# Linear attention's reciprocals: spread over the heads' rows by a matmul, or loaded with repeats

## The chip, the cores and the metric

The kernel runs on one core of one Trainium2 chip. The metric is the device time of one execution in microseconds (us), the median of several runs. The engines of the core are named as in the profile: PE (TensorE, matmul), PEld (its weight loads), DVE (VectorE), ACT (ScalarE), POOL (GpSimd), SP (SyncE, which here only issues DMAs).

## What is computed

A decoder layer on x of 2 x 2048 rows by 512: linear attention, cross attention to 154 context rows, and a mixture of 8 experts of which 6 are used, plus a shared one. Each part is normalised ahead and added to x. The change touches the end of the first part:

```python
q_proj = _elu1(jnp.einsum('bhnd,hdf->bhnf', q, proj_matrix))
k_proj = _elu1(jnp.einsum('bhnd,hdf->bhnf', k, proj_matrix))
kv = jnp.einsum('bhnf,bhnd->bhfd', k_proj, v)
attn = jnp.einsum('bhnf,bhfd->bhnd', q_proj, kv)
k_sum = k_proj.sum(axis=2)
z = 1.0 / (jnp.einsum('bhnf,bhf->bhn', q_proj, k_sum) + 1e-08)
attn = attn * z[..., None]
out = attn.transpose(0, 2, 1, 3).reshape(b, n, d)
return out @ w_out + b_out
```

There are 16 heads of 32 columns. For each head and token there is one denominator, and its reciprocal z multiplies that head's 32 numerators.

## The kernel before

The 4096 rows are cut into 8 blocks of 512 tokens (`TB`); blocks 0 to 3 are the first batch (`bpb` is 4), 4 to 7 the second. A tensor of a block is held transposed, as 4 chunks of 128 columns (4 heads of 32) by 512 tokens. Large products are made of pairs, a high part that the matmul takes exactly and a low rest, as three matmuls (`product`, L144). `low` (L116) makes the rest by a subtraction.

SBUF is handed out by pools. `big` has 17 buffers of 8 KB per partition (`eight`), which hold weights, loaded queries (`qst`), numerators (`num`), the attended pairs (`at`), and so on; `work` has among others 4 buffers `hl` for pairs (`pair_of`). PSUM has 8 banks: 4 in pool `ps` (`bank`), for products of all kinds, and 4 in pool `sc`, for features and scores. A scheduler of the tile framework puts the instructions of each engine in an order when the kernel is built; engines and DMA queues then work in that order, and a tile that takes over a buffer waits for the last reader of the one before. Nearly all DMAs are issued by SP; the numerators and the cross attention's keys by POOL.

The stages that matter here:

- The loop at L1306 makes the key features of all blocks, and, two steps behind, the query features, numerators and denominators of blocks 0 to 3. `numerators` (L485) stores those of blocks 0 to 3 to DRAM (`numd`), while those of blocks 4 to 7 stay in SBUF. In block 7 of this loop the cross attention's weights, w_out, the first numerators and the first reciprocals are loaded.
- The loop at L1346 goes over the 16 chunks of blocks 4 to 7 (`steps`): it loads queries (`load_queries`), makes their features (matmul `pqp`, then Relu and Exp on ACT and a sum on DVE: `features`, L361), numerators (`pn`) and denominators (`pd`). Between them it deals out the finishing of blocks 0 to 6: `ahead` gives each step a block and a pair of chunks, for which `attended` is called, two calls a step. After a block's last chunk its `attention_out` (L567) is added to the fill work: four times 12 matmuls `po_a`, an addition of x's rows (`xr_a`) and a store to x1.
- The loop at L1390 is the cross attention of all blocks (scores `psc`, Exp on ACT). In its first block, block 7 of the linear attention is finished in the same way.
- The experts follow, from about 1075 us to the end.

The way of a denominator: `denominators` (L507) sums into one bank `pd` per block; `reciprocals` (L522) adds 1e-8 on DVE (`den`), stores it to DRAM (`dd`, four DMAs), loads it back over 128 partitions (`z`, `turned`), takes the reciprocal there and stores it to DRAM again (`zd`, `stored`). `load_reciprocals` (L548) then loads for two chunks, by four DMAs, each head's row 32 times into the 32 partitions of that head (`zr`, in an `hl` buffer). `attended` (L558) multiplies the numerators by it on POOL, in place (the trace names that operation num<-num,zr), copies the result to the high part on ACT, and makes the low part on DVE.

Of the kernel before, what the change touches and what calls it, by code (L numbers as in the profile page):

```python
# [17 lines left out]
P = 128  # L18
# [12 lines left out]
Z_EPS = 1e-8  # L31
LAG = 3
SC = 4
GROUP = 2


@with_exitstack
def decoder_layer(
# [59 lines left out]
    def eight(shape, dtype, name):  # L98
        return big.tile(shape, dtype, tag="b8", name=name)
# [4 lines left out]
    def pair_of(name, n=TB):  # L104
        return work.tile([P, 2, n], FR, tag="hl", name=name, bufs=4)
# [361 lines left out]
        dense.add(*tr[:1], query_chunk(b, 0), *ln[3:], *tr[1:2], key_chunk(b, 3))  # L467
        dense.add(*tr[2:3], query_chunk(b, 1), *tr[3:], query_chunk(b, 2), query_chunk(b, 3))

    qsts, qps, pds, nums, numd, zrs, zds, ats = {}, {}, {}, {}, {}, {}, {}, {}  # L470

    def load_queries(b, c):
        qsts[b, c] = eight([3 * HD, 4, TB], FR, f"qst{b}_{c}")
# [48 lines left out]
    def reciprocals(b, pd):  # L522

        den = half(f"den{b}")
        nc.vector.tensor_scalar(den, pd, Z_EPS, None, ALU.add)
        dd = dram.tile([4, NC, TB], F32, name=f"dd{b}")
        for h in range(4):
            nc.sync.dma_start(out=dd[h], in_=den[h * HD : h * HD + NC, :])
        z = small.tile([P, H * TB // P], F32, tag="z", name=f"z{b}", bufs=1)
        flat = "h c n -> (h c n)"  # L530
        zd = dram.tile([4, NC, TB], F32, name=f"zd{b}")

        def turned():
            nc.sync.dma_start(out=z, in_=dd.rearrange(flat).rearrange("(p n) -> p n", p=P))

        def stored():
            tc.keep_in_program_order(nc.vector.reciprocal(z, z))
            nc.sync.dma_start(out=zd.rearrange(flat).rearrange("(p n) -> p n", p=P), in_=z)

        dense.after(10, turned)  # L540
        dense.after(26 if b < nblk - 1 else 24, stored)
        zds[b] = zd
# [2 lines left out]
        nums[b] = eight([P, NC, TB], F32, f"num{b}")  # L545
        nc.gpsimd.dma_start(out=nums[b], in_=numd[b])

    def load_reciprocals(b, c):  # L548
        two = pair_of(f"zr{b}_{c}").bitcast(F32)
        for h in range(4):  # L550
            nc.sync.dma_start(
                out=two[h * HD : (h + 1) * HD],
                in_=zds[b][h : h + 1, c : c + 2].to_broadcast([HD, 2, TB]),
            )
        for i in range(2):
            zrs[b, c + i] = two[:, i]

    def attended(b, c):  # L558

        if c == 0:  # L560
            ats[b] = [eight([P, NC, TB], FR, f"at{b}_{i}") for i in range(2)]
        at = nums[b][:, c]
        nc.gpsimd.tensor_tensor(at, at, zrs.pop((b, c)), ALU.mult)
        nc.scalar.copy(ats[b][0][:, c], at)
        low(ats[b][1][:, c], at, ats[b][0][:, c])

    def attention_out(b, t):  # L567
        if not 0 <= b < nblk:
# [737 lines left out]
    for n in range(nblk * per):  # L1306
        b, c, t = n // per, n // NT % NC, n % NT
        dense.fill(58 if n == 0 else fl(n, 9.25) if n < 32 else fl(n, 9.5))
        if (b, c, t) == (nblk - 1, 0, 0):
            context_load()  # L1310
        if (b, c, t) == (nblk - 1, 1, 0):
            xwk = split_weight(wk_t, "xwk")
            dense.add(*(context_key(i, xwk) for i in range(NC)))
        if (b, c, t) == (nblk - 1, 2, 0):
            xwv = split_weight(wv_t, "xwv")
            bvr = half("bvr")
            nc.sync.dma_start(out=bvr, in_=bv.to_broadcast([P, D]))
            for bt in range(batches):
                dense.add(*(context_value(bt, at, xwv, bvr) for at in range(0, keys, P)))
        if (b, c, t) == (nblk - 1, 3, 0):  # L1320
            load_numerators(0)
            load_reciprocals(0, 0)
            bout = load_row(b_out, "bout")
        dense.until(stks, (b, c))
        key_features(b, c, t)
        todo.append((b, c, t))
        m = n - bpb * per - shift
        if m == -4:
            load_queries(0, 0)
        if m >= 0:  # L1330
            query_step(m)
        if n % 2 and len(todo) > LAG:
            sums_step(m)
# [12 lines left out]
    for n in range(len(steps) + 1):  # L1346
        if n < len(steps):
            b, c = steps[n]
            if n + 1 < len(steps):
                load_queries(*steps[n + 1])  # L1350
        if n + 1 in ahead:
            load_reciprocals(*ahead[n + 1])
        if n == 7:
            ln, tr = layernorm(x1[0], 0, 0, qts, "x")
            dense.add(*ln[:3])
            ln = ln[3:]
        if n == 8:
            dense.add(*tr[:1], *ln, *tr[1:])
        if n == 11:
            dense.add(*(cross_query(0, i) for i in range(NC)))  # L1360
        for i in range(2):
            if n < len(steps):
                query_features(b, c, 2 * i)
                query_features(b, c, 2 * i + 1)
            dense.fill(fl(2 * n + i, 13 if n < 12 else 14))
            if n in ahead:
                attended(ahead[n][0], ahead[n][1] + i)
                if ahead[n][1] and i:
                    whole = ahead[n][0]
                    if whole < nblk - 2:  # L1370
                        dense.add(*attention_outs(whole))
                    if whole + 1 < bpb:
                        load_numerators(whole + 1)
            if n and i:
                columns.batch()
                numerators(*steps[n - 1])
                denominators(*steps[n - 1])
        if n == 10:
            xwq = split_weight(wq_t, "xwq")
        if n == 11:  # L1380
            open_early.clear()
            attending.close()
            res = attending.enter_context(tc.tile_pool(name="res", bufs=1))
            for i in range(NC):
                load_keys(0, i)
# [4 lines left out]
    for n in range(len(steps) + LAG + 1):  # L1390
        if n < len(steps):
            b, c, t = steps[n]
            k = NT * c + t
            dense.until(xsts, (b, c))
            scores(b, c, t)
            if b == 0:
                if k == 0:
                    load_values(0)
                if k in (NC - 1 + 0, NC + 1 + 0):
                    load_reciprocals(nblk - 1, k - 0 - NC + 1)  # L1400
                if NC + 0 <= k < 2 * NC + 0:
                    attended(nblk - 1, k - NC - 0)
                if k == 8:
                    bor = load_row(bo, "bor")
                    xwo = split_weight(wo_t, "xwo")
            if b == 0 and k == 0:
                ln, tr = layernorm(x1[1], 1, 0, qts, "x")
                outs = [[attention_out(nblk - i, t) for t in range(NT)] for i in (2, 1)]
                new = [cross_query(1, i) for i in range(NC)]
                kinds = {"L": ln, "a": outs[0], "T": tr, "b": outs[1], "q": new}  # L1410
                dense.add(*(kinds[x].pop(0) for x in "LLLaTLTaTTaaqbqbqbqb"))
            if k == LAG + 0 and b:
                outs = [cross_out(b - 1, i) for i in range(NT)]
                new = [cross_query(b + 1, i) for i in range(NC)]
                if b + 1 < nblk:
                    ln, tr = layernorm(x1[b + 1], b + 1, 0, qts, "x")
                    kinds = {"L": ln, "o": outs, "T": tr, "q": new}
                    dense.add(*(kinds[x].pop(0) for x in "LLLoTLTTToqoqoqq"))
                else:
                    dense.add(outs[0], tr[0], ln[3], outs[1], *tr[1:])  # L1420
            if b == nblk - 1 and k == 1:
                ln, tr = expert_ahead(0)
                dense.add(*ln[:3])
                load_unit(0)
            if b == nblk - 1 and k == 9:
                ln, tr = expert_ahead(1)
                ready = products(0)
                dense.add(prepare(0, 0), *ln[:3], tokens_part(0, 0), tokens_part(0, 1))
                dense.add(tr[0], ready[0], ln[3], *tr[1:], ready[1], *outs[2:])
            dense.fill(fl(k, 9.5 if b == 0 else 7.75 if b < nblk - 1 else 5.5))  # L1430
            if b % bpb == bpb - 1 and b + 1 < nblk and c > 0 and t == 1:
                load_keys(b // bpb + 1, c - 1)
            if b % bpb == 0 and b and k == 0:
                load_keys(b // bpb, NC - 1)
        if LAG <= n < len(steps) + LAG:
            turn(*steps[n - LAG])
        if n > LAG:
            b, c, t = steps[n - LAG - 1]
            if t == NT - 1:
                values(b, c)  # L1440
                if c == NC - 1 and (b + 1) % bpb == 0 and b + 1 < nblk:
                    load_values((b + 1) // bpb)
# [180 lines left out]
```

## Time and profile before

| what | value |
|---|---|
| median of 3 runs | 2324.54 us (2317.61 to 2330.41) |
| the profiled execution | 2323.77 us, its span 2321.7 us |
| busy, share of the span | PE 2234.2 us (96%), DVE 72%, POOL 53%, ACT 47% |
| bytes moved | 498.23 MB, 215 GB/s over the span |
| stretch 430 to 480 us | PE busy 41.8 of 50 us, granted clock 0.90, DMA engines 94% busy |
| stretch 480 to 660 us | PE busy 159.7 of 180 us, granted clock 0.96, DMA engines 89% busy |
| stretch 660 to 720 us | PE busy 58.4 of 60 us, granted clock 0.99, DMA engines 74% busy |
| stretch 720 to 1075 us | PE busy 336.3 of 355 us, DMA engines 58% busy |
| stretch 1075 to 2322 us | PE busy 1227.4 of 1247 us, DMA engines 62% busy |

The loop over the 16 chunks (L1346) runs from about 495 to 645 us, with its loads beginning at about 445 us; the experts are over half of the span. A row of the profile that names a group of instructions gives its line, engine, operation, and the tiles written and read (out<-in); a helper's line, such as L118 for `low`, stands for all its callers, so tile names tell them apart. An arrow in a table of waits points at what ended the wait.

### The profile page before, as it was taken

How to read it: one execution, taken by the hardware profiler on the slowest of the kernel's cores; microseconds unless marked ns; L12 is line 12 of the kernel's file. 1: busy time of each engine (PE TensorE's matmuls, PEld its weight loads, DVE VectorE, ACT ScalarE, POOL GpSimd, SP SyncE). 2: the span in 40 equal slices, each digit the busy share in tenths (PEclk: the TensorE clock that was granted, in tenths of full speed). 3: DMA queues.
4: the chain of work that ended last, by engine and by line, in shares of the span. 5: the costliest groups of instructions: out<-in, count | busy, mean ns of one | idle time of the engine just before them, and what ended most of it. 6: DMA issues, size and time to landing. Idle time of an engine off the chain costs nothing.

```text
span 2321.7 us, 35182 instructions
## 1 busy us (share of the span) xinstructions
PE 2234.2 (96%) x11978; PEld 1733.5 (75%) x11978; DVE 1675.2 (72%) x2733; ACT 1101.6 (47%) x2598; POOL 1225.3 (53%) x1078
## 2 busy tenths in 40 slices
PE   7999999898989999999999999999999999999999
PEld 5888777645667777766787877888878888788887
DVE  6554555568587777878877776788787887877777
ACT  4555677656466676765343343222433223432221
POOL 5555333446475565554766454555474554755443
PEclk9999999989999999999999999999999999999999
DMA  7656777889975665666867557665547666575553
GB/s 213 182 169 176 201 219 215 248 235 278 249 216 153 171 183 170 183 183 223 287 237 260 216 185 292 226 232 226 195 168 281 231 231 235 196 281 204 209 190 132
DMA packets 201809, 498.23 MB, mean 215 GB/s; under 512 B 27738, under 2 KB 47578, under 8 KB 181694
## 3 DMA queue, kind: packets, MB, share of 16 engines
q1 hardware_dynamic: 199902, 489.89, 64.2%
q0 software_dynamic: 1728, 6.09, 0.9%
q8 instruction: 96, 1.57, 0.3%
q14 instruction: 83, 0.68, 0.1%
HBM read 351.30 MB, written 144.60 MB: 214 GB/s over the span
## 4 chain that ended last, share of the span: by engine, by line
PE 73%; DMA 12%; DVE 6%; issue 3%; ACT 2%; POOL 2%; SPq 1%; DVEq 0%; ACTq 0%; POOLq 0%
PE pg L1082 30%; PE pf L1195 11%; PE pf L148 4%; PE pk L148 3%; PE pv L148 3%; PE pq L148 3%; PE po_x L148 3%; PE xpq L148 2%; PE pp L402 2%; PE pc L745 1%; PE pkv L230 1%; PE psc L693 1%; DMA qst<-qd 1%; PE xpt L725 1%; ACT xe L703 1%
## 5 line engine op out<-in xcount | busy, mean ns | idle before, releaser
L1082 PE MATMUL pg<-xo,wq 128*128 128x512 f32 x3360 | 823.2, 393 | 3.4 <-DVE xo L118 1.4
L1082 PEld LDWEIGHTS pg<-xo,wq 128*128 128x128 f32 x3360 | 630.4, 188 | 143.0 <-DVE xo L118 3.4
L407 POOL TENSOR_TENSOR kacc<-kacc,e_k 128x512 f32<-128x512 f32 x128 | 166.0, 1297 | 225.4 <-DVE e_k L366 206.3
L1216 DVE TENSOR_TENSOR sum<-sum,pf 128x512 f32<-128x512 f32 x376 | 251.2, 683 | 45.9 <-PE pf L1195 41.3
L703 ACT ACTIVATE xe<-psc,nb 128x154 f32<-128x154 f32 x512 | 195.2, 417 | 87.5 <-DVE nb L700 81.7
L708 POOL TENSOR_TENSOR xe<-xe,sm 128x616 f32<-128x616 f32 x128 | 157.7, 1237 | 93.6 <-DVE sm L707 61.3
L1195 PE MATMUL pf<-ht,wdo 128*128 128x512 f32 x696 | 185.5, 393 | 4.9 <-DVE sum L1216 3.2
L1145 POOL TENSOR_TENSOR u<-u,gr 128x512 f32<-128x512 f32 x48 | 65.1, 1356 | 227.3 <-DVE u L1114 226.6
L366 DVE SCALAR_TENSOR_TENSOR e_k<-pp,e_k 128x512 f32<-128x512 f32 x128 | 87.4, 684 | 108.5 <-ACT e_k L365 102.4
L1113 ACT ACTIVATE u<-u 128x512 f32<-128x512 f32 x80 | 50.6, 633 | 231.6 <-DVE u L1102 231.5
L1195 PEld LDWEIGHTS pf<-ht,wdo 128*128 128x128 f32 x696 | 130.8, 188 | 35.7 <-issue 3.3
L1195 PE MATMUL pf<-hb,wdo 128*128 128x512 f32 x522 | 146.8, 398 | 1.0 <-DVE sum L1216 0.9
L148 PE MATMUL pf<-wd,hp 128*128 128x512 f32 x528 | 135.1, 403 | 5.4 <-DVE mv_n L248 3.4
L148 PEld LDWEIGHTS pf<-wd,hp 128*128 128x128 f32 x528 | 100.2, 192 | 34.6 <-issue 6.5
L700 DVE TENSOR_REDUCE nb<-psc 128x2 f32<-128x308 f32 x256 | 111.3, 464 | 12.0 <-PE psc L693 11.8
L703 ACT ACTIVATION_READ_ACCUMULATOR xe<-psc,nb 128x1 f32 x512 | 118.3, 231 | 0.0
L1102 DVE TENSOR_TENSOR u<-u,pg 128x512 f32<-128x512 f32 x160 | 107.9, 680 | 13.5 <-PE pg L1082 12.5
L1195 PEld LDWEIGHTS pf<-hb,wdo 128*128 128x128 f32 x522 | 97.2, 188 | 24.8 <-DVE sum L1216 3.6
L364 ACT ACTIVATE e_k<-pp 128x512 f32<-128x512 f32 x128 | 76.8, 601 | 69.5 <-PE pp L402 62.5
L693 PE MATMUL psc<-xkst,xst 96*128 96x154 f32 x512 | 91.8, 286 | 11.7 <-ACT xe L703 10.8
L693 PEld LDWEIGHTS psc<-xkst,xst 96*128 96x128 f32 x512 | 77.7, 193 | 27.1 <-ACT xe L703 18.0
L402 PEld LDWEIGHTS pp<-pst,kst 96*128 96x128 f32 x512 | 76.1, 192 | 27.8 <-issue 5.8
(285 smaller groups left out, 5118.7 us busy)
## 6 DMA issues: line engine op xcount, KB each, us to landing
wq<-wqs SPq DMA_DIRECT2D x90, 1024.0 KB
wqs<-wq SPq DMA_DIRECT2D x30, 1024.0 KB
wdo<-wds SPq DMA_DIRECT2D x29, 1024.0 KB
kst<-kd SPq DMA_DIRECT2D x96, 256.0 KB
qst<-qd SPq DMA_DIRECT2D x96, 256.0 KB
xst<-xqd SPq DMA_DIRECT2D x96, 256.0 KB
wdo<-wds SPq DMA_DIRECT2D x29, 768.0 KB
kd<-khl SPq DMA_DIRECT2D x32, 512.0 KB
```

The source lines that it names most:

```text
L148: nc.tensor.matmul(dst, lhsT=a, rhs=b, start=n == 0, stop=n == len(todo) - 1)
L366: nc.vector.scalar_tensor_tensor(e, src, 0.0, e, ALU.max, ALU.add)
L402: nc.tensor.matmul(pp[:, h], lhsT=stks[b, c][:, h, rows], rhs=pst[:, head], start=True, stop=True)
L407: nc.gpsimd.tensor_tensor(acc, acc, kp, ALU.add)
L693: nc.tensor.matmul(psc[:, i], lhsT=xsts[b, c][:, h, t * P : (t + 1) * P], rhs=ksts[bt, c][:, h, :], start=True, stop=True,)
L700: nc.vector.tensor_reduce(nb[:, two], psc, AX.X, ALU.max, negate=True)
L703: nc.scalar.activation(e[:, h, :], psc[:, i], AF.Exp, bias=nb[:, h : h + 1], accum_out=sm[:, h : h + 1],)
L708: nc.gpsimd.tensor_tensor(e, e, sm.unsqueeze(2).to_broadcast([P, 4, keys]), ALU.mult)
L1082: nc.tensor.matmul(pb, lhsT=w[:, p, i, k, :], rhs=xop[:, q, k, :], start=first and m == 0, stop=m == len(todo) - 1, skip_group_check=True,)
L1102: nc.vector.tensor_tensor(dst, dst, pb, ALU.add)
L1195: nc.tensor.matmul(banks[i], lhsT=w[:, p, i * P : (i + 1) * P], rhs=t[q], start=new and m == 0, stop=m == len(TERMS) - 1, skip_group_check ...
L1216: nc.vector.tensor_tensor(dst, dst, banks[i], ALU.add)
```

## The change

The reciprocals are no longer loaded with repeats. `stored` makes a pair of them, high and low part, and stores both (`zd` is twice as large). One DMA per block (`load_reciprocals`) brings the block's 2 x 16 rows of 512 tokens to 32 partitions of a new buffer `spread`, in one of 3 places that take turns. `spread` also holds, written once by `spread_setup`, a matrix of zeros and ones that says which rows belong to which of the 128 columns of a chunk. `attended` begins with one matmul by it, which puts each head's reciprocal (high plus low part) on its 32 rows of a bank `pz` of pool `ps`; DVE multiplies the numerators by that bank, ACT copies the high part as before, and POOL makes the low part. The numerators of a first-batch block are loaded two blocks ahead (block 1's together with block 0's), where it was one.

```diff
-        z = small.tile([P, H * TB // P], F32, tag="z", name=f"z{b}", bufs=1)
+        zhl = small.tile([P, 2, H * TB // P], FR, tag="z", name=f"z{b}", bufs=1)
+        z = zhl[:, 1].bitcast(F32)
...
-        zd = dram.tile([4, NC, TB], F32, name=f"zd{b}")
+        zd = dram.tile([2, 4, NC, TB], F32, name=f"zd{b}")
...
             tc.keep_in_program_order(nc.vector.reciprocal(z, z))
-            nc.sync.dma_start(out=zd.rearrange(flat).rearrange("(p n) -> p n", p=P), in_=z)
+            nc.scalar.copy(zhl[:, 0], z)
+            low(zhl[:, 1], z, zhl[:, 0])
+            nc.sync.dma_start(
+                out=zd.rearrange("r h c n -> r (h c n)").rearrange("r (p n) -> p r n", p=P),
+                in_=zhl.bitcast(F32),
+            )
...
-    def load_reciprocals(b, c):
-        two = pair_of(f"zr{b}_{c}").bitcast(F32)
-        for h in range(4):
-            nc.sync.dma_start(
-                out=two[h * HD : (h + 1) * HD],
-                in_=zds[b][h : h + 1, c : c + 2].to_broadcast([HD, 2, TB]),
-            )
-        for i in range(2):
-            zrs[b, c + i] = two[:, i]
+    spread = []
+
+    def spread_setup():
+        both = eight([P, 1 + SPREAD, TB], FR, "spread")
+        nc.gpsimd.memset(both.bitcast(F32), 0.0)
+        rows = [
+            ident[: 2 * H, r * H : (r + 1) * H]
+            .rearrange("p (h c) -> p c h", h=4)
+            .unsqueeze(3)
+            .to_broadcast([2 * H, NC, 4, HD])
+            for r in range(2)
+        ]
+        to = both[: 2 * H, 0].rearrange("p (c h d) -> p c h d", c=NC, h=4)
+        nc.vector.tensor_tensor(to, *rows, ALU.add)
+        spread.append(both)
+
+    def load_reciprocals(b):
+        nc.sync.dma_start(
+            out=spread[0][: 2 * H, 1 + b % SPREAD].bitcast(F32),
+            in_=zds[b].rearrange("r h c n -> (r h c) n"),
+        )
...
+        pz = bank(f"pz{b}_{c}")
+        nc.tensor.matmul(
+            pz,
+            lhsT=spread[0][:, 0, c * P : (c + 1) * P],
+            rhs=spread[0][:, 1 + b % SPREAD],
+            start=True,
+            stop=True,
+        )
         at = nums[b][:, c]
-        nc.gpsimd.tensor_tensor(at, at, zrs.pop((b, c)), ALU.mult)
+        nc.vector.tensor_tensor(at, at, pz, ALU.mult)
         nc.scalar.copy(ats[b][0][:, c], at)
-        low(ats[b][1][:, c], at, ats[b][0][:, c])
+        low(ats[b][1][:, c], at, ats[b][0][:, c], nc.gpsimd)
...
             load_numerators(0)
-            load_reciprocals(0, 0)
+            load_numerators(1)
+            spread_setup()
+            load_reciprocals(0)
+            load_reciprocals(1)
...
-        if n + 1 in ahead:
-            load_reciprocals(*ahead[n + 1])
+        if n + 1 in ahead and not ahead[n + 1][1] and ahead[n + 1][0] > 1:
+            load_reciprocals(ahead[n + 1][0])
...
-                    if whole + 1 < bpb:
-                        load_numerators(whole + 1)
+                    if whole + 2 < bpb:
+                        load_numerators(whole + 2)
...
-                if k in (NC - 1 + 0, NC + 1 + 0):
-                    load_reciprocals(nblk - 1, k - 0 - NC + 1)
+                if k == NC - 1:
+                    load_reciprocals(nblk - 1)
```

More of the change, by code (lines that the diff above doesn't have):

```diff
@@ L33 @@
 SC = 4
+SPREAD = 3
 GROUP = 2
@@ L468, in decoder_layer @@
         dense.add(*tr[2:3], query_chunk(b, 1), *tr[3:], query_chunk(b, 2), query_chunk(b, 3))
-    qsts, qps, pds, nums, numd, zrs, zds, ats = {}, {}, {}, {}, {}, {}, {}, {}
+    qsts, qps, pds, nums, numd, zds, ats = {}, {}, {}, {}, {}, {}, {}
     def load_queries(b, c):
```

## The prediction

> **What bounds the kernel now.** I read the page first, then a table of stretches, then the chain of waits and the waits themselves in the stretch that the change touches. The page says that TensorE (PE) is busy for 96% of the span, so a change can only gain where PE is not. The table of 20 us stretches finds that place. Its columns are the stretch, its length, the busy us (and instructions) of PE, PEld, DVE, ACT and POOL, the granted PE clock, the busy share of the DMA engines, and GB/s.
>
> ```profile
> 460.00:480.00 20.00, 16.62 (x133) 10.63 (x132) 13.60 (x22) 14.89 (x30) 7.36 (x7) 0.83 0.99 282
> 480.00:500.00 20.00, 17.99 (x89) 7.54 (x88) 12.37 (x22) 7.63 (x15) 10.08 (x9) 0.91 0.76 220
> 520.00:540.00 20.00, 17.00 (x85) 10.12 (x83) 14.70 (x22) 11.47 (x21) 10.31 (x8) 0.97 0.95 278
> 620.00:640.00 20.00, 18.07 (x93) 12.48 (x93) 9.18 (x15) 9.02 (x17) 2.53 (x2) 1.00 1.04 283
> 640.00:660.00 20.00, 12.98 (x76) 8.86 (x69) 16.13 (x36) 10.93 (x46) 10.51 (x13) 0.87 0.68 176
> 660.00:680.00 20.00, 20.00 (x120) 16.73 (x122) 16.14 (x33) 12.52 (x52) 17.47 (x14) 0.96 0.72 213
> 460.00:660.00 200.00, 176.36 (x932) 107.50 (x931) 141.42 (x227) 116.46 (x241) 104.90 (x98) 0.94 0.90 249
> ```
>
> Between 460 and 660 us PE is idle for 200 - 176.4 = 23.6 us while the DMA engines are 90% busy and no other compute engine is above 71%. The clock loses more: one minus the granted clock, times PE's busy time, summed over the ten stretches, is 9.3 us (2.8 of it in the first). From 660 us on PE is full again. So some 33 us are open here, and DMA is the suspect. The chain of waits over these 200 us (whose line the view cuts off) agrees, and the waits name what is late (us in total, times, longest):
>
> ```profile
> by line: issue 13.4%; DMA qst<-qd 9.0%; DMA zr<-zd 8.3%; DMA xr_a<-in_x 6.8%; DMA xst<-xqd 6.6%; DMA x<-xr_a 6.3%; DMA num<-numd 4.7%; DVE at L118 4.3%; PE xpq L148 4.2%; POOL num L563 3.6%; DMA zd<-z 2.5%; DVE xr_a L315 2.5%; DMA dd<-den 2
> ACT at L564 <- POOL num L563: 33.2, 15, 6.7
> POOL num L563 <- DMA zr<-zd: 27.7, 4, 17.0
> DVE at L118 <- ACT at L564: 22.9, 6, 7.7
> POOL num L563 <- DMA num<-numd: 17.6, 3, 8.8
> PE pqp L479 <- DVE e_q L366: 8.1, 6, 2.8
> zr<-zd SPq DMA_DIRECT2D x60, 128.0 KB
> ```
>
> The reader is to see a relay: POOL's multiplication waits for the reciprocals (zr) or the numerators (num), ACT's copy waits for POOL, and behind ACT's copy in its queue stand the Exp and Relu of the features (e_q), whose banks PE waits for. The last line, from the DMA issues between 430 and 660 us, counts 60 loads of zr: 7.9 MB of the 57.9 MB moved there.
>
> **The change part by part.** All sums are against the profiled execution, span 2321.7 us, 2323.8 with what lies around it; the median of the runs, 2324.5, is 0.7 above that. I add the differences to the median.
>
> *Added on PE.* 32 matmuls pz (8 blocks of 4), 128x512 like those of po_a. A dozen of these takes 2.80 us:
>
> ```profile
> 664.66 2.80 PE po_a L148 x12
> ```
>
> That is 0.233 us each from start to start, so 32 x 0.233 = 7.5 us, on PE's path since nothing else runs there meanwhile. Each pz also takes one of the four banks of `ps`. The nearest row is pn, which shares them: its weight loads waited 2.1 us in 4 cases for the bank of an out (DVE xr_a), for 16 pn. For 32 pz that is 4.2 us at most; PE itself was idle for 0.5 us of it, so 1.0. I take 1.0, ends 0 and 4.2.
>
> *Swapped.* Per chunk POOL's multiplication (mean 1422 ns there) and DVE's subtraction (mean 1134 ns) become DVE's multiplication out of a bank (DVE xr_a L315, also out of a bank: 674 ns) and POOL's subtraction (POOL's wout_lo, the same operation: 1293 ns). DVE is relieved by 32 x 0.46 = 14.7 us, POOL by 4. The relay itself is 1.42 + 0.62 + 1.13 = 3.2 us before and 0.23 + 0.67 + 0.62 + 1.29 = 2.8 after: no gain taken on the path. POOL's subtraction stands in a queue with the additions xr_a, which waited 24.1 us for their loads; a late one now holds back the low half, and po_a after it.
>
> *Setup.* One memset of 128x2048 on POOL (kacc's: 1890 ns) and one DVE operation on 32 rows (under 0.68 us), near 445 us. POOL is idle for 4.3 us there before its next kacc: cost nothing; without that cover 1.9 us. Per block there is one ACT copy and one DVE subtraction of 128x64 more (the reciprocal of that shape takes 548 ns): 8 x about 1.1 us, not on PE's path but in the chain from den to pz, which is costed under the rivals.
>
> *Removed.* 64 loads of zr, 8 of 64 KB come instead. Of the 57.9 MB, 7.9 - 0.3 (spread) - 0.2 (zd doubled) = 7.4 MB or 12.7% go away. The gain has three parts, each with both ends. First, zr's own share of the chain, 8.3% of 200 = 16.6 us, at three places (462, 588 and 636 us). A small load stands there instead: xkst, 77 KB, lands in 3.4 us, so 3 x 3.4 = 10.2 and the gain is 6.4 (0 to 16.6). Second, the numerators two blocks ahead: 4.7% of 200 = 9.4; their megabyte has to move all the same, num1's now at 445 us beside w_out's loads where the DMA share is 0.97, so I take half, 4.7 (0 to 9.4). Third, the other transfers of the chain (qst, xr_a, xst, x, zd: 31.2% or 62.4 us) go through a queue that carries 12.7% less: 7.9 us if its rate alone sets them, and half, 4.0, as many are set by the order of SP's queue (0 to 7.9). Together 15.1 of the 23.6 us of idle time. What is late next are the features' banks (8.1 us of waits for e_q) and xr_a.
>
> *Clock.* After idle spells the granted clock falls: in 475 to 479 us PE was busy 3.0 of 4 us, with one gap of 1.2 us, and the next 4 us got 0.71. So idle time given back gives back clock: 9.3 x 15.1 / 23.6 = 6.0 us (0 to 9.3).
>
> The Trainium skill speaks against this term: its page "TensorE: Matmul & The Clock Gate" (Part 1, the HAM clock gate) says that the clock is halved only after an idle window of about 3.4 us. No gap of PE between 460 and 660 us is that long (the longest has 3.1 us), so by the rule the term would be nothing and the time some 2318. The row above shows losses after shorter gaps, and I go by the row.
>
> *Buffers.* `spread` and the second numerator hold 2 of the 17 slots of `big`. In the changed order of instructions each qst's slot comes free 21 to 43 us of PE work ahead of its use, before 26 to 54; its load takes some 6 us. Nothing taken.
>
> Sum: +7.5 + 1.0 - 15.1 - 6.0 = -12.6 us: 2324.5 - 12.6 = 2312. Best end: all of PE's idle time and clock, 32.9, less 7.5: 2299.
>
> **The rivals.**
> *No change to speak of.* The idle time stays and moves to other releasers: the page shows DVE and ACT in the same relay, and SP's queue hands out loads in order, whoever is fast. For it: PE's own idle time is written mostly to e_q, not to zr. Against it: these e_q are late behind ACT's copy, which waits for POOL and so for zr. With the three gains at a third (5.0, clock 2.0): 2324.5 + 8.5 - 7.0 = 2326; its range is 2313 to 2336.
>
> *Slower: PE stops at pz.* Before, a late reciprocal stopped POOL, and PE met it only at po_a. Now pz stands in PE's own queue, and everything behind it waits: the next features, scores and outs. Block 5's den was made at 574.2 us and POOL began on its reciprocals at 593.8: 19.6 us. In the changed order PE's work between the last pd and the first pz, at the row's prices, is 50, 40, 23.3, 22.2 and 15.4 us for blocks 3 to 7. If the chain grows by 5 us (zd<-z is 5.0 us of it, at 582 us in the chain of waits, and becomes twice as large), it is 24.6, and PE waits 1.3 + 2.4 + 9.2 = 12.9 us, and some 3.5 more by the clock (three times 4 us at 0.71). With no relief of the queue this gives 2324.5 + 8.5 + 16.4 = 2349, with half of it 2339. It decides from a chain above about 23 us. Against it: zd's store shares the queue that is relieved, and block 7 has scores on ACT in its stretch (four Exp per tile, each 0.42 us and 0.23 for reading its sum, 8 tiles: 21 us), so that PE is late there by itself.
>
> The Trainium skill has a rule for this rival: "DMA: Bandwidth & Descriptors" (Specifications) wants transfers of at least 512 B. The store's rows are 256 B before and stay so, twice as many; by the rule the store's 5.0 us would come near 10, which is the growth that the rival supposes on other grounds.
>
> *More than forecast.* The gains go to their best ends: 2299, the floor that PE's work sets.
>
> **How the numbers follow.** Half a per cent, 11.6 us, is about what a measurement of this kernel can tell from no change. The forecast 2312 with the better rival: 0.50. Little or no change: 0.35. Slower by a stop at pz: 0.15. The likeliest time is 2312, its own range 2299 to 2320. To hold 8 in 10 the range goes to 2334, so that of the middle case nearly all is in it and of the slower one nothing.
>
> **What would show it.** In the profile after: pz at about 0.233 us a piece; POOL's 27.7 and 17.6 us of waits for zr and num gone; PE idle between 460 and 660 us below 10 us and the clock there above 0.96; bytes moved down by about 8 MB; PE unchanged from 1075 us on. Wrong would be: PE or its weight loads waiting for spread by several us, above all at pz of blocks 5 to 7 (then slower), or the same 20 us of idle time behind e_q, qst or xr_a (then no change).

## The result, and the profile after

| | before | after |
|---|---|---|
| median (range), 9 runs each | 2322.82 (2313.16 to 2330.41) | 2334.52 (2331.84 to 2338.68) |
| ratio to before, 95% interval | 1 | 1.0051 (1.0038 to 1.0064) |
| profiled execution, span | 2323.8, 2321.7 | 2338.7, 2337.0 |
| bytes moved | 498.2 MB | 490.1 MB |

The change makes the kernel 11.7 us slower, where 12 us faster was forecast. A second set of runs beside other kernels gave 1.0053 (1.0037 to 1.0069). The profiled execution of the changed kernel is the slowest of its nine, 4 us above their median.

First the stretches, from the profile after (stretch, length, busy us and instructions of PE, PEld, DVE, ACT and POOL, granted PE clock, DMA share, GB/s), and one line of the kernel before for the stretch that the prediction had not shown:

```profile
460.00:660.00 200.00, 184.51 (x1014) 118.09 (x1013) 137.28 (x235) 118.97 (x245) 102.72 (x100) 0.97 0.80 222
640.00:660.00 20.00, 15.29 (x80) 9.30 (x72) 15.12 (x31) 9.90 (x39) 13.04 (x15) 0.83 0.43 117
660.00:680.00 20.00, 14.00 (x61) 11.53 (x62) 10.49 (x27) 9.88 (x45) 13.42 (x12) 0.74 0.45 133
...
640.00:740.00 100.00, 82.97 (x468) 60.39 (x460) 64.84 (x144) 56.58 (x232) 57.81 (x57) 0.86 0.52 148
```

```profile
640.00:740.00 100.00, 88.48 (x536) 67.86 (x532) 77.87 (x168) 62.94 (x256) 66.41 (x64) 0.95 0.65 187
```

From 460 to 660 us things went the way that was forecast, if less far: PE's idle time fell from 23.6 to 15.5 us, and the DMA share from 0.90 to 0.80. But behind it PE does 468 instructions in 640 to 740 us where it did 536, at a clock of 0.86 where it had 0.95. From 660 to 680 us, where PE had been full, it is now idle for 6.0 us, with 0.74 of the clock in the rest: that is 6.0 + 0.26 x 14.0 = 9.6 us.

To see where the time of a kernel goes, I cut its trace at instructions that every kernel here has: the end of DVE's copy of the 9th numerator chunk (385 us before), of the 32nd (650), of ACT's first write of `xh_x` of cross block 3 (778), and the start of the first `pg` of the experts (1041). The last column ends with the start of the last `pg`; the time ahead of the first cut (385 to 389 us) and the last 22 to 23 us stand in no column. From about the third cut on, PE's instructions have one and the same order in all of these kernels, so what differs in the last two parts is no matter of PE's order.

| us between the cuts | linear attention | cross attention's start | rest of it | experts |
|---|---|---|---|---|
| before | 265.4 | 127.6 | 263.3 | 1258.9 |
| after | 263.8 | 138.5 | 261.9 | 1263.2 |
| after, second trace | 263.1 | 137.5 | 266.7 | 1257.6 |

The second part is where the loss is: 10 to 11 us, between 650 and 778 us. Some 3 us of that (an estimate from po_a's 0.233 us) are work that only changed sides: at the second cut the changed kernel is 20 matmuls behind (ten po_a, four transposes, six scores), and does them in the second part. Both parts together are 9.3 and 7.6 us longer. The variants of the changed kernel below have the same shift, so it doesn't touch comparisons among them. In the second part block 7's outs are finished among the scores of the first cross block. What happens there is seen in the chain of waits of the kernel after (start, us, what):

```profile
657.27 0.26 DVE nb L729
...
662.80 4.50 DMA x<-xr_a
...
667.36 0.33 SPq L288
...
667.78 2.84 DMA zd<-z
...
670.64 1.75 DMA spread<-zd
...
672.52 0.77 PE pz L584
```

The chain leaves PE at 657 us and comes back at 672.5, and it comes back through block 7's reciprocals: their store zd, their load spread, and pz. The DMAs as SP issues them (start, us, line, what) show why they are late:

```profile
652.92 1.30 SPq L529 DMA_DIRECT2D dd<-den  x4
654.33 6.85 SPq L679 DMA_DIRECT2D vbd<-vd  x8
661.22 0.55 SPq L536 DMA_DIRECT2D z<-dd  x1
...
664.49 3.20 SPq L288 DMA_DIRECT2D xsxwo<-in_wo_t  x2
667.78 0.39 SPq L542 DMA_DIRECT2D zd<-z  x1
...
670.64 0.33 SPq L574 DMA_DIRECT2D spread<-zd  x1
```

The denominators leave at 652.9, but the read that turns them stands behind eight loads of vbd, and the store zd behind loads at L288, one of which waits in SP's queue until x<-xr_a has landed at 667.3. From den to pz it is 20 us. That is not new: in the kernel before, the read of dd also stood behind loads of vbd (six of the eight), and POOL began to multiply by block 7's reciprocals at 671.5 us, about when the first pz runs here:

```profile
659.32 0.48 SPq L534 DMA_DIRECT2D z<-dd  x1
```

```profile
671.47 2.53 POOL L563 TENSOR_TENSOR num<-num,zr 128x512 f32<-128x512 f32 x2
```

From 660 us on PE was busy all that while. What is new is that PE's own queue now holds an instruction that needs them. PE's own rows (start, us, line, what, and in brackets the idle time ahead and who ended it) show how this looks from PE:

```profile
665.00 0.65 PE L722 MATMUL psc<-xkst,xst 96*128 96x154 f32 x4
670.13 0.71 PE L722 MATMUL psc<-xkst,xst 96*128 96x154 f32 x2 [4.48 <-ACT xe L732]
671.35 0.71 PE L722 MATMUL psc<-xkst,xst 96*128 96x154 f32 x2 [0.52 <-ACT xe L732]
672.52 0.77 PE L584 MATMUL pz<-spread 128*128 128x512 f32 x1 [0.46 <-DMA spread<-zd]
...
679.40 0.43 PE L149 MATMUL xpq<-xh_x,xwq_hi 128*128 128x512 f32 x1
```

Only 0.46 us of idle time is put down to the reciprocals (1.35 in the second trace); the 4.48 us ahead (3.12) are put down to ACT's Exp. ACT stood for POOL's normalisation of the scores, and that stood in POOL's queue behind an addition that waited for its load:

```profile
666.76 1.26 POOL L313 TENSOR_TENSOR xr_a<-xr_a,bout 128x512 f32<-128x512 f32 x1 [4.60 <-DMA xr_a<-in_x]
```

That wait by itself need not stop PE: the kernel below with block 7's reciprocals on chip and its low halves on DVE has it too (4.47 us, up to 662.1 us), and there PE stands for 1.5 us of it only, since it has outs to do. Here the instructions stand in an order that was fixed when the kernel was built, with the reciprocals' lateness in it (a kernel below differs in that dependence alone, and has another order). Score matmuls that wait for ACT stand ahead of pz, and behind it stands what could have filled the hole: block 6's last out and the second cross query, xpq, which was made at 672 to 675 us before and now starts at 679.4. So a late input can show as a wait of whatever the order has put in front of it.

In the waits of 460 to 660 us (engine, line, waited for; us in total, times, longest) POOL no longer waits for zr or num; it waits for xr_a's loads (24.1 us before) and for ACT's copy ahead of its new subtraction:

```profile
POOL xr_a L313 <- DMA xr_a<-in_x: 42.1, 13, 8.7
POOL at L119 <- ACT at L593: 38.3, 9, 17.6
ACT at L593 <- DVE num L592: 35.3, 18, 9.1
```

PE's own waits there changed too. For e_q it waits 2.0 us, where it waited 8.1; two kinds are new, pz for a bank that the addition xr_a has still to read, and po_a for POOL's low half (4.8 and 1.3 us in the second trace):

```profile
PE pz L584 <- DVE xr_a L316: 3.9, 1, 3.9
PE po_a L149 <- POOL at L119: 3.4, 2, 2.4
```

### The profile page after: what moved, and what is told of

Its sections match the earlier page's. It is cut to its first block, busy times and chain, and to the rows that moved or that the text cites. A ratio compares the mean times of both kernels' runs of the same rounds, so it can differ in the third digit from the quotient of the medians.

```text
span 2337.0 us, 35166 instructions
## 1 busy us (share of the span) xinstructions
PE 2245.6 (96%) x12010; PEld 1742.1 (75%) x12010; DVE 1668.9 (71%) x2742; ACT 1102.4 (47%) x2606; POOL 1218.6 (52%) x1079
## 4 chain that ended last, share of the span: by engine, by line
PE 72%; DMA 12%; DVE 7%; issue 3%; ACT 3%; POOL 2%; SPq 1%; DVEq 0%; ACTq 0%; POOLq 0%
PE pg L1111 30%; PE pf L1224 11%; PE pf L149 5%; PE pq L149 3%; PE pk L149 3%; PE pv L149 3%; PE po_x L149 3%; DMA xsx<-x 2%; PE pp L403 2%; PE pc L774 2%; DMA qst<-qd 1%; PE pkv L231 1%; PE xpq L149 1%; PE po_a L149 1%; DMA xqd<-xhl 1%
```

## The experiments

Ratios are to the kernel before on the same chip, with their 95% intervals; 0.1% is 2.3 us. In a code cut, three dots stand for lines left out. Each variant is scheduled anew, so an edit also moves other instructions up to some 778 us; a difference below some 3 us is not read as an effect of the edit.

**Block 7 by the old path.** The changed kernel with

```diff
+        if b == nblk - 1:
+            at = nums[b][:, c]
+            nc.gpsimd.tensor_tensor(at, at, zrs.pop((b, c)), ALU.mult)
+            nc.scalar.copy(ats[b][0][:, c], at)
+            low(ats[b][1][:, c], at, ats[b][0][:, c])
+            return
...
```

and the loads of zr for block 7, whose zd is single again.

> The changed kernel, but the last block (7) gets its reciprocals by the old way: loads of zr, POOL's multiplication, DVE's low half; blocks 0 to 6 keep pz. Theory A (blocks 0 to 6 break even, and the loss of about 12 us arises where block 7 is finished inside the first block of cross attention): about 10 us below the changed kernel, 2322 to 2326, equal to the kernel before. Rival B (the loss is the 28 pz of the other blocks and 7 idle places that the traces of one execution hide): unchanged, 2332 to 2336, less at most 1 us for four pz.

0.9990 (0.9977 to 1.0003), as theory A has it: block 7's new path costs 0.61%, 14 us, and without it the change is level with the kernel before. The part from 650 to 778 us takes 125.3 us.

**Block 7 alone by the new path**, in the kernel before:

```diff
...
+                if k == NC - 1:
+                    load_spread(nblk - 1)
-                if k in (NC - 1 + 0, NC + 1 + 0):
-                    load_reciprocals(nblk - 1, k - 0 - NC + 1)
```

> The kernel before, but block 7 alone gets its reciprocals by the new way (spread set up at the same place, one load, four pz, DVE's multiplication, POOL's low half); numerators one ahead. Theory A: block 7 alone brings the loss, about +10 us on the kernel before, 2330 to 2336. Rival B: four pz cost 1 us, 2322 to 2326.

1.0023 (1.0011 to 1.0036), 5 us: more than rival B has, half of what A has. In its trace PE's hole ahead of the first pz of block 7 is 1.05 us. From 650 to 778 us it takes 128.3 us, only 0.7 more than the kernel before, so alone in the old order the new path does less harm there; the trace doesn't show where its 5 us arise.

**Block 7's low halves on DVE**, in the changed kernel:

```diff
-        low(ats[b][1][:, c], at, ats[b][0][:, c], nc.gpsimd)
+        low(ats[b][1][:, c], at, ats[b][0][:, c], None if b == nblk - 1 else nc.gpsimd)
```

> The changed kernel, but block 7's low halves are on DVE, as before, and not on POOL. If POOL's subtractions amid the scores' normalizations are what costs (their four took 1257 to 1454 ns each, with the additions xr_a that wait for loads in the same queue): 4 to 10 us below the changed kernel, 2325 to 2331. If the cost lies in pz and its chain, or in the order of the work: within 3 us of the changed kernel, 2332 to 2337.

1.0018 (1.0006 to 1.0031), 7.7 us below the changed kernel: the four subtractions on POOL matter.

**Block 7 without waiting for its reciprocals**:

```diff
-            rhs=spread[0][:, 1 + b % SPREAD],
+            rhs=spread[0][:, 1 + min(b, nblk - 2) % SPREAD],
```

> The changed kernel, but block 7's pz reads the place of block 6's reciprocals, so it waits for nothing of its own chain (den, z, zd, spread; these are still made and loaded). Leaves out: block 7 is multiplied by block 6's reciprocals. The prediction's slower rival (PE stops at pz of block 7 because the chain is late): 9 us or more below the changed kernel, 2320 to 2326. If the chain is not what is late there (the trace has 0.46 us of idle time of PE before the first pz of block 7): within 3 us of the changed kernel, 2332 to 2337.

0.9985 (0.9971 to 0.9998), 15 us below the changed kernel. PE's rows and its stretch in this kernel:

```profile
660.82 0.43 PE L584 MATMUL pz<-spread 128*128 128x512 f32 x1
...
664.84 0.51 PE L584 MATMUL pz<-spread 128*128 128x512 f32 x1
665.18 0.40 PE L149 MATMUL xpq<-xh_x,xwq_hi 128*128 128x512 f32 x1
```

```profile
660.00:680.00 20.00, 19.82 (x121) 15.45 (x120) 14.43 (x37) 16.48 (x69) 18.93 (x16) 1.00 0.63 191
```

With nothing late, pz stands ahead, xpq fills 665 to 668 us, and the hole is gone: PE is busy for 19.8 of 20 us at the full clock. Taking the dependence away, with the order that comes of it, is worth 15 us, where the profile showed a wait of 0.46. POOL's low halves are still there, so beside an early pz they need not cost anything.

**vbd's loads behind the read of dd**, the changed kernel again beside it, and both mends together. In the trace of the first, six of the eight loads come behind that read:

```diff
-                if k == 0:
+                if k == 2:
                     load_values(0)
```

> The changed kernel once more, beside the next three on one chip, as their reference. 2332 to 2337, ratio 1.004 to 1.006; much lower would mean that the first four experiments were compared with an unlucky number.

> The changed kernel, but the eight loads of vbd, which stand in SP's queue ahead of block 7's read of dd (654.3 to 661.2 us in the changed kernel's trace), are asked for two tiles later, behind that read. Nothing is left out. Theory C (block 7's reciprocals are late, and PE's order puts pz and all that follows it, the second cross query xpq among it, behind score matmuls that wait for ACT): the chain comes some 6 us sooner, xpq and po_a move ahead, and the loss is mostly gone: 2322 to 2327. Rival D (it is POOL's or ACT's work for block 7 that costs, whenever it comes): within 3 us of the changed kernel, 2331 to 2337.

The changed kernel: 1.0053 (1.0037 to 1.0069). With vbd later: 1.0021 (1.0008 to 1.0034), 7.4 us better, about half of the loss. zd is now stored at 663.3 us instead of 667.8 and spread issued at 666.4 instead of 670.6, the order has pz ahead of the scores of the third chunk, and now the wait shows at pz itself:

```profile
670.59 0.60 PE L584 MATMUL pz<-spread 128*128 128x512 f32 x1 [3.42 <-DMA spread<-zd]
```

> The changed kernel with both small mends of block 7: vbd's loads behind the read of dd (0.32% by itself) and its low halves on DVE (0.33% by itself). If lateness and POOL's place are two causes: 12 to 18 us below the changed kernel, 2319 to 2325 or a ratio of 0.998 to 1.000. If they are one and the same: 6 to 9 us below it, ratio 1.001 to 1.003.

1.0012 (1.0002 to 1.0022): 9 us below the changed kernel, as the second reading has it. The two mends (7.4 and 7.7) do not add up, so here lateness and POOL's place are largely one cause: on top of the first the second gives some 2 us.

**Block 7's reciprocals without DRAM.** DVE takes them on den itself, and ones in den's lanes spread them:

```diff
+        if b == nblk - 1:
+            nc.vector.reciprocal(den, den)
+            hi, lo = spread[0][:, 1 + b % SPREAD], spread[0][:, 1 + (b + 1) % SPREAD]
+            nc.scalar.activation(hi, den, AF.Copy, scale=spread[1])
+            nc.vector.scalar_tensor_tensor(lo, den, spread[1], hi.bitcast(F32), ALU.mult, ALU.subtract)
+            return
...
```

`spread[1]` is a column of ones and zeros that keeps the lanes in use.

> The changed kernel, but block 7's reciprocals never go through DRAM: DVE takes them on den itself (128x512, where the turned form has 128x64 and took 0.55 us; by eight times the columns some 4 us, an estimate), ACT and DVE split them into two halves in spread, and two accumulating pz per chunk spread them with ones in the lanes of den. Computes the same as the reference. Chain from den to pz: 4 + 0.6 + 0.7, about 6 us, in place of 20. Theory C (the lateness of block 7's reciprocals is the loss): as with block 6's reciprocals in their place, 2319 to 2325, which is 12 to 16 us below the changed kernel. Rival D (the work on DVE, ACT and POOL for block 7 costs whenever it comes): 2330 to 2337.

1.0023 (1.0011 to 1.0035): 7 us below the changed kernel, not the 12 to 16 of theory C. The chain itself is ready 8.5 us after den was begun, where it takes 20 in the changed kernel (DVE's rows):

```profile
649.92 0.67 DVE L526 TENSOR_SCALAR den<-pd 128x512 f32<-128x512 f32 x1
...
651.71 3.31 DVE L528 RECIPROCAL den<-den 128x512 f32<-128x512 f32 x1
...
657.69 0.73 DVE L531 SCALAR_TENSOR_TENSOR spread<-den,mask,spread 128x512 fp32r<-128x512 f32 x1
```

So lateness alone, taken away in this way, is half of the loss. An early chain is not yet an early pz: in the order made for this kernel the first pz of block 7 stands 16.7 us behind the last numerator copy, against 21.3 in the changed kernel and 14.0 in the one that doesn't wait. The next run takes the other edit with it; below, its kernel is called the mended one.

> The same with block 7's low halves on DVE in place of POOL. If POOL's place of the low half is a cost of its own, beside the chain: 3 to 8 us below the run before it, 2313 to 2320. If it mattered only because the chain was late: within 3 us of it.

0.9986 (0.9972 to 1.0001), 8.6 us better than without the second edit: POOL's place of the low half is a cost of its own here, as the first of the two readings said. The first pz stands as far behind as before (16.7 us), and the part from 650 to 778 us takes 125.3 us, where it took 131.8 with POOL's low halves. In the waits of the kernel with POOL's low halves PE stands once there, at 722 us, for DVE behind a chain through xsx's loads; the other kernel has no such wait:

```profile
PE po_x L149 <- DVE cx L119: 4.0, 1, 4.0
```

How POOL's four subtractions lead to that wait was not followed. Once more:

> The kernel with block 7's reciprocals on chip and its low halves on DVE, once more: 0.9986 of the kernel before with an interval that just takes in 1. If it beats the kernel before, 0.997 to 0.9995 again.

0.9985 (0.9967 to 1.0002). Both medians lie 1.7 and 3.0 us under those of the kernel before and both ratios under 1, by about what can be told from no change; it undoes the loss, and it is not shown to be a gain. In the traces its first two parts together are 5.0 and 7.0 us shorter than those of the kernel before (388.0 and 386.0 against 393.0), and the rest is longer.

**The price of pz**, on the changed kernel and on the mended one (28 more there):

```diff
+        for _ in range(2):
             nc.tensor.matmul(
                 pz,
...
```

> The changed kernel with every pz done twice into the same bank, 32 matmuls more. It measures the price of pz, which the prediction has at 0.233 us each, on PE's path: 7.5 us above the changed kernel, 2341 to 2346. If pz lies in idle time of PE that is there anyway: 0 to 3 us, 2332 to 2338.

> The same kernel with every pz of blocks 0 to 6 done twice (28 matmuls more): the price of pz where block 7 isn't late. The prediction's price: 28 times 0.233 = 6.5 us above that kernel, 2330 to 2334. If PE isn't what sets the end of this stage: 0 to 2 us, 2322 to 2326.

1.0054 (1.0035 to 1.0072), no more than the changed kernel's 1.0051 and 1.0053; and 1.0001 (0.9989 to 1.0014) where the mended kernel has 0.9986 and 0.9985, which is 3.5 us. By the medians a second pz thus costs nearly nothing where block 7 is late, and half of its 0.233 us where it isn't; in that second case the intervals are wide enough for the full 6.5 us too.

**The relief.** The kernel before with zr loaded once (the cut below); the same with block 7 loading its own; and the mended kernel with zr's 60 loads put back, unread:

```diff
+        if b:
+            for i in range(2):
+                zrs[b, c + i] = every[0][:, c + i]
+            return
...
```

> The kernel before, with zr loaded for block 0 only and kept in one slot of big; blocks 1 to 7 are multiplied by block 0's reciprocals. Leaves out: the loads of the other blocks' reciprocals (56 of 64) and the waits for them. It shows what the relief of the DMA engines is worth by itself, without pz and without the swap of engines. The prediction's sum (15.1 us of idle time and 6.0 of clock): 17 to 21 us below the kernel before, 2303 to 2308. The rival (the idle time stays behind e_q, qst and xr_a): 0 to 8 us below, 2316 to 2324.

> The kernel before, with zr loaded for blocks 0 and 7 only; blocks 1 to 6 are multiplied by block 0's reciprocals, block 7 by its own, loaded where it was. Leaves out: the loads of blocks 1 to 6 and the waits for them. From the first score matmuls on, every engine's order is that of the kernel before. If the run with zr loaded once lost its relief (3.5 us in its trace up to the last numerators) because block 7 came at another time and moved the scores' order: 4 to 16 us below the kernel before, 2308 to 2320. If idle time given back up to 660 us is lost again whatever block 7 does: within 4 us of it, 2320 to 2328.

> The kernel of the run with block 7's reciprocals on chip and its low halves on DVE (0.9986 of the kernel before), with the 60 loads of zr of blocks 0 to 6 put back, into tiles that nothing reads. Only the load on the queues and on the DMA engines comes back, no wait for it. The prediction's relief (15.1 us of idle time and 6.0 of clock): 10 to 20 us above that kernel, 2334 to 2344. If the idle time that the relief gives back in 460 to 660 us is lost again behind it, as the run with zr loaded once suggests: within 4 us of it, 2320 to 2328.

1.0023 (1.0010 to 1.0035), 0.9998 (0.9983 to 1.0013), and 1.0079 (1.0063 to 1.0094). Taken out of the kernel before, the loads bring no gain, though the linear attention itself gets 3.5 and 5.3 us shorter in the traces (261.9 and 260.1 us between the first two cuts; two traces of one kernel differ by up to 2.6 us there). Both runs also keep one of the 17 buffers of `big` for the reciprocals, as spread does. Put back onto the mended kernel the loads cost some 21 us, about what the prediction had for them; 6 to 8 of these lie ahead of 650 us in the traces (268.6 against 262.7 and 260.1). They also take `hl` buffers again, which the run doesn't part from the load on the DMA engines. The line of 460 to 660 us of the kernel with loads for blocks 0 and 7 alone, and of the one with the loads put back:

```profile
460.00:660.00 200.00, 181.96 (x962) 113.31 (x954) 143.51 (x229) 114.84 (x241) 106.51 (x98) 0.95 0.79 220
```

```profile
460.00:660.00 200.00, 178.18 (x950) 110.19 (x949) 132.62 (x217) 110.28 (x219) 93.02 (x90) 0.96 0.93 254
```

The first has PE idle for 18.0 us, where the kernel before has 23.6; the second for 21.8, where the mended kernel has 17.2 and 16.6. So the loads are behind some 5 us of idle time in this stretch and not 15. What the rest of the 21 us is was not settled: 8 lie in 650 to 778 us, 11 behind it, where the order of PE's work is the same, against 4 in the other direction in the experts. By these runs the relief has no one price: nothing in the kernel before, 21 us in the mended one.

**Numerators one ahead, and all low halves on DVE**, in the changed kernel:

```diff
-            load_numerators(1)
...
-                    if whole + 2 < bpb:
-                        load_numerators(whole + 2)
+                    if whole + 1 < bpb:
+                        load_numerators(whole + 1)
```

> The changed kernel with numerators loaded one block ahead, as before. The prediction's term for the second block ahead is 4.7 us (0 to 9.4), so 2337 to 2344. If the numerators come in time either way once zr's loads are gone: 2332 to 2336, and if the megabyte at 445 us beside w_out's loads costs: 2328 to 2332.

1.0057 (1.0041 to 1.0073): 0.9 us above the changed kernel's 1.0053, which is no difference that can be told.

```diff
-        low(ats[b][1][:, c], at, ats[b][0][:, c], nc.gpsimd)
+        low(ats[b][1][:, c], at, ats[b][0][:, c])
```

> The changed kernel with all low halves on DVE, as before the change. The prediction took nothing for the swap of engines. If that holds: within 3 us of the changed kernel for blocks 0 to 6, and what block 7 alone gave (8 us) still there: 2324 to 2331. If the relief of DVE (32 times 0.46 us) was worth something in blocks 0 to 6: 2331 to 2340.

1.0039 (1.0025 to 1.0053), above the 1.0018 of block 7's alone: by the medians the swap to POOL was worth 5 us for blocks 0 to 6, and cost 8 for block 7. Both differences are between ratios from different sets of runs, each to the kernel before beside it; the intervals of the first pair overlap, so the 5 us are not shown.

| us between the cuts | linear attention | cross attention's start | rest of it | experts |
|---|---|---|---|---|
| block 7 old | 259.9 | 125.3 | 263.3 | 1263.7 |
| low halves of 7 on DVE | 259.4 | 133.9 | 261.3 | 1262.1 |
| no wait for 7's | 259.1 | 124.3 | 261.0 | 1263.5 |
| vbd later | 265.1 | 132.1 | 266.0 | 1262.6 |
| without DRAM | 262.8 | 131.8 | 261.4 | 1264.7 |
| the same, low on DVE | 262.7 | 125.3 | 260.0 | 1263.4 |
| that, second trace | 260.1 | 125.9 | 261.9 | 1263.4 |
| zr once | 261.9 | 134.3 | 266.6 | 1259.5 |
| zr for 0 and 7 | 260.1 | 129.1 | 268.8 | 1256.4 |
| zr put back | 268.6 | 133.2 | 270.9 | 1258.9 |

The first two columns carry the effects (the trace of the kernel with vbd later is its slowest execution, 5.6 us above the median). The third scatters from 260.0 to 270.9 us although the order is the same, and the last two together are 1522.2 us in the one trace of the kernel before and 1523.4 to 1529.8 in all others. So a single trace can't settle a few microseconds there; verdicts above rest on the medians.

## Why the prediction was wrong

- **pz, 7.5 us on PE's path.** Mis-sized by the medians: doubling it costs nearly nothing in the changed kernel, 3.5 of 6.5 us in the mended one. Its duration was about right (0.27 us from start to start at the full clock); that nothing else covers it did not hold where block 7 is late, and is not settled elsewhere.
- **Bank waits, 1.0 us (0 to 4.2).** 4.5 us: one wait of 3.9 us ahead of a pz, until the addition `xr_a` had read its bank, and one of 0.6. They lie from 640 to 660 us, a stretch in which PE's idle time fell from 7.0 to 4.7 us all the same.
- **The swap, nothing on the path.** By the medians some 5 us gained in blocks 0 to 6 (not shown beyond the intervals), 8 lost in block 7. The prediction named the queue (POOL's subtraction behind the additions xr_a) and gave it no price; po_a waits 3.4 us for POOL's low half up to 660 us.
- **The removed loads, 15.1 us, and the clock, 6.0.** PE's idle time in 460 to 660 us fell by 8.1 us and the clock rose from 0.94 to 0.97, but 28 pz at 0.233 us take 6.5 of the 8.1, and blocks 0 to 6 with all of it leave the kernel at 0.9990. In the kernel before the relief alone brings no gain. The waits named (27.7 and 17.6 us of POOL) are gone as forecast. The rival of no change had the idle time move to other releasers, and in part it did: not to e_q, whose 8.1 us fell to 2.0, but to the bank of xr_a and to POOL's low half. Of the numerators' 4.7 us nothing can be told from none. (The trace has 68 loads of zr, not 64: block 0's first two chunks are loaded twice.)
- **The slower rival is what happened, at one of its three places.** It had block 7 late by 9.2 us plus clock, from a chain of 24.6 us against 15.4 us of PE's work. The chain is 20 us, the hole 5.5 us with 0.74 of the clock, and undoing it gives 14 to 15 us. Blocks 5 and 6 don't wait. Its point of decision was put at 23 us, where blocks 5 and 6 begin to wait; for block 7 its own figure was 15.4, and the 19.6 us that the prediction had measured for block 5 were beyond that with no growth at all. Nor did the chain grow by the store's rows: zd, 5.0 us for block 5 before, took 2.84 here with twice as many. SP's queue makes it long (z's read behind vbd, 6.9 us; zd behind the loads at L288, 2.7 us).

The step that failed is the one that put block 7's wait at pz at nothing and the rival at 0.15: that block 7 has scores on ACT in its stretch, so that PE is late there by itself. In the kernel before PE is busy for 20.00 of 20 us from 660 to 680, with fill work (the outs and xpq) laid between the scores. pz in PE's order takes this fill away from the place where it was needed: PE is idle for 6.0 us there, and with nothing late ahead of pz the kernel gets 15 us back. The stretch was in the prediction's own first view, as the place where PE is full, and was not asked what keeps it full.

The wrong sign thus comes from a term that was left out (14 us), and the missing gain from a sum over idle time that took it as time saved.

## What to carry to other kernels

An instruction that is put into the queue of the busiest engine brings its input's lateness there: ask what the order will put behind it, not how long it waits. The wait in the profile (0.46 us) says little of that; a run with the wait's cause taken away says it (15 us). And look for the price of a moved input in the queue that issues its DMAs: at the seam of two stages other loads stand there, and two small moves (six loads behind one, a chain kept off DRAM) got 7 us each.

## What the runs showed of the hardware that was not expected

- DVE's reciprocal takes 0.55 us on 128x64 and 3.31 us on 128x512, so 6.2 ns for each further column.
- SP's eight issues of vbd took 6.85 us, 0.86 us each, where the load of spread took 0.33 us to issue and landed 1.75 us after its issue began. The Trainium skill's page "DMA: Bandwidth & Descriptors" (Issuing engines are not separate DMA queues) calls the time to initiate a DMA usually small beside the DMA. No run here shows how long one load of vbd took, but eight in a row held up the small read behind them for longer than the whole load of spread.
- After the gap of 4.48 us a run of po_a went at half pace: a group of three takes from 676.93 to 678.21 us, 0.43 us each, and from 684.43 to 685.13, 0.23 each, later. About 8 us of such pace followed a hole of 5 us. The Trainium skill's page "TensorE: Matmul & The Clock Gate" (Part 1) has the half clock after an idle window of about 3.4 us, which agrees with this gap; the 0.71 that the prediction read after gaps of at most 1.2 us does not follow from it.
- With the same order of PE's instructions from 778 us on, the rest of the cross attention took between 260.0 and 270.9 us in different kernels. PE is idle for 7.4 us of the shortest and 15.1 us of the longest (at scores that wait for ACT 3.0 and 6.9 us), and the granted clock there is 1.00 and 0.99. Why ACT is later in one than in the other was not found.
